# Attention over the kept tokens, one core: the first batch's side work in other slots, batch six's output products over three slots, the last pair's short chunk second and its outputs chunk by chunk

## The chip, the core and the metric

The kernel runs on one core of one Trainium2 chip. The metric is the device time in microseconds of one execution. Every number below comes from three timed executions of the kernel before the change, or from one profiled execution of it, in which each instruction and each DMA packet carries a time.

The engines are named as in the profile: PE (matrix multiplication; PEld is its weight load), DVE (vector), ACT (scalar, with the exponentials), POOL (general, here mostly the issuer of indirect DMAs) and SP (which only issues DMAs). Each works through its own list of instructions in order; semaphores tie the lists together.

## The reference

Eight batches of 512 features by 1024 tokens, eight heads of 64 features, a 0/1 mask over the tokens that keeps about half of them:

```
xt = transpose(x, (0, 2, 1))
q = xt @ Wq.T
qh = q.reshape(B, T, 8, 64).transpose(0, 2, 1, 3)
scores = scale * einsum('bhqd,bhkd->bhqk', qh, qh)
logits = (scores * cmask + (1.0 - cmask) * NEG) * rmask
attn = softmax(logits, axis=-1)
ctx = einsum('bhqk,bhkd->bhqd', attn, qh)
out = ctx.transpose(0, 2, 1, 3).reshape(B, T, D) @ Wo.T
return x + transpose(out, (0, 2, 1))
```

Query, key and value are the same projection. A masked token attends to all tokens alike, so all masked tokens of a batch have one output row. Only the kept tokens (at most 536 here) and one row for the mean have to be computed.

## The kernel before

**Tiling.** Per batch the tokens are turned into rows in DRAM (`turn`: a DVE transpose of a quarter of the batch, then four DMAs by SP). The rank of each kept token is looked up (`search`, DVE), the kept rows are gathered by indirect DMA (`gather`, POOL), and PE transposes them back into feature-major form (`collect`, five chunks, copied out of PSUM by DVE or ACT). `add_features` sums features on ACT. The heads go in pairs, four pairs per batch, 32 pairs in all, written here as (batch, pair). A pair's 536 tokens are four long chunks of 128 and a short one of 24, number 4, called `LAST`.

**The loop.** For each pair there are five slots, c = 0 to 4. A slot issues `scores` of its chunk (PE, then ACT's exponentials with a running sum: two of 128x536 for a long chunk, the tiles `e`, two of 128x268 for the short one, the tile `el`), then the products of earlier chunks' exponentials with the values (`weigh`, PE, tiles `av`), and side work that a table puts there: `put(batch, pair, slot, task, rank)`. Tasks of a slot with a rank below 0 come before `weigh`, those from 0 to 5 after it, those from 5 up last. The engines' lists keep this order.

**Side work that the change moves.** For the pair after the one running: `project` (queries), `turn_values` (values through PE and two copies by DVE), `square` (ACT) of the values, `top_of` (DVE: the sums of the squares, `len`, and their maximum, `top`), `bias_of` (PE spreads `top`, DVE makes of it the bias that the next pair's exponentials need). So in slot 4 there is a chain: square (ACT), len and top (DVE), top (PE), bias (DVE), first exponential of the next pair (ACT).

**The gate.** `open_slot` and `pass_gate` make the first `weigh` of a slot wait for the first noted read of a PSUM bank since the slot before, or else for the slot's own first exponential. In slot 4 that is mostly the short chunk's first `el`.

**PSUM.** The pool tag "t" has two banks, used in turn by nearly all side work of PE; the scores have two tiles of two banks ("s"), the products with the values two banks ("av").

**Outputs.** A batch's output is made by seven half-size products after Strassen's scheme (`half_product` k = 1 to 7, tiles `ph`) and a plain one for the short chunk (`output`). DVE combines them into `side` and `joined` tiles, reading `ph` out of the "t" banks; `joined_0` and `joined_1` are the two halves of the rows and go to DRAM (`od`) by POOL's DMAs. Later POOL fetches all 1024 tokens' rows with indirect DMAs that add to the input rows (`fetch`, eight per batch, blocks i = 0 to 7), DVE transposes each block (`finish_blocks`, tile `whole`) and SP stores it. For batch five the fetches stand in the slots of pair (7,0) and the blocks in those of (7,1); for batch six everything stands in (7,1) to (7,3).

**The end.** The last batch's outputs are plain products, four per chunk, one per pair. Three of the four (`begin_output`) stand in the last pair's slots 3 and 4 and are kept in SBUF as partial sums; after the last pair `end_output` adds the fourth on DVE and stores the chunk. `fetch_last` gathers the eight blocks from `od`, and `finish_tokens` transposes them on PE, adds x on DVE, and stores.

Of the kernel before, what the change touches and what calls it, by code (L numbers as in the profile page):

```python
# [305 lines left out]
def attention_of_kept_tokens(ctx, tc, x, mask, wq, wo, out, ident, wqT, woT, verdict, flag):  # L306
# [416 lines left out]
    def weigh(pair, c, cross):  # L723
# [7 lines left out]
        for r in range(2):  # L731
            rows = slice(r * DK, (r + 1) * DK)
            hf = r ^ cross
            for h in range(2):
# [5 lines left out]
                    stop=(c == LAST),  # L740
# [3 lines left out]
    def weigh_behind(pair, before, c):  # L744


        cross = c in (2, 4)
# [236 lines left out]
    def last_products(b, i, prs, po):  # L984

        n = max(Q, sizes[i])
        for pr in prs:
            first, last = pr == prs[0], pr == prs[-1]
# [19 lines left out]
    def begin_output(b, i):  # L1008
# [5 lines left out]
        partials[i] = pa  # L1014

# [71 lines left out]
    def fetch(b, i):  # L1087
        nc.gpsimd.indirect_dma_start(  # L1088
            out=gs[b, i],
            out_offset=None,  # L1090
            in_=ods[b],
# [242 lines left out]
    def plan():  # L1334
# [15 lines left out]
        for p, (b, pr) in enumerate(pairs[:-1]):  # L1350
# [4 lines left out]
            put(b, pr, 3, squares, ahead, rank=0)  # L1355
# [3 lines left out]
        for n in range(1, B):  # L1359
            if n == 1:  # L1360
                turns = [(0, 0, 0), (0, 0, 1), (0, 0, 3), (0, 0, 4)]
                finds = [(0, 1, 0), (0, 1, 3), (0, 1, 3), (0, 1, 4), (0, 2, 0)]
                feats = [None] * (ND + 2) + [(0, 0, 4), (0, 1, 0)]
                takes = finds
                means, mean = (0, 2, 1), (0, 2, 3)
                turned = [(0, 2, 3)] * NC
            else:
                b = n - 2
                if n == 2:
                    loads = [(0, 1, i) for i in range(NC)] + [(0, 2, i) for i in range(3)]  # L1370
                    turns = [(0, 2, 3), (0, 2, 4), (0, 3, 1), (0, 3, 3)]
                    feats = [(0, 2, 3)] * 2 + [(0, 2, 4)] * 2
# [19 lines left out]
            for i in range(NQ):  # L1392
                put(*turns[i], turn, n, i, rank=6.8 if turns[i][2] == LAST - 1 else 1)
# [3 lines left out]
            for i in range(NC):  # L1397
                put(*finds[i], search, n, i, rank=4.6 if n > 1 and finds[i][2] == LAST else 0)
# [8 lines left out]
        for b in range(B - 1):  # L1407
# [3 lines left out]
            if b == B - 3:  # L1411
                steps = ((1, 2), (6, 5, LAST + P), (7, 3, 4))
            elif b == B - 2:
                steps = ((1, 2, 6, 5, 4, 7, 3, LAST + P),)
            for i, step in enumerate(steps):
                for k in step:
                    task, k = (output, k - P) if k > P else (half_product, k)
                    put(*at[i], 3, task, b, k, rank=7.1)
                    if b == B - 2 and task is half_product and k == 5:
                        for j in (2, 3):  # L1420
                            put(*at[i], 3, mix_contexts, b, j, rank=7.1)
# [5 lines left out]
            else:  # L1427
                for k in range(2):
                    put(nxt, 1, 1 + k, mix_contexts, b, k, rank=5.5)
            if b < B - 3:  # L1430
# [23 lines left out]
        last = B - 1  # L1454
        for i in (LAST, 0, 1, 2):
            put(last, 3, 3 + (i == 2), begin_output, last, i, rank=7)
        for k in range(ND):
            put(*((0, 3, 1), (0, 3, 2), (0, 3, 3), (1, 1, 2))[k], mix_weights, k, rank=5.5)
# [10 lines left out]
    def late(n):  # L1469
# [41 lines left out]
        for p, pair in enumerate(pairs):  # L1511
# [3 lines left out]
            for c in range(NC):  # L1515
# [159 lines left out]
```

## Time and profile before

| | us |
|---|---|
| median of three executions | 635.94 |
| lowest, highest | 634.38, 639.89 |
| profiled execution, whole | 637.8 |
| profiled execution, its span from first to last instruction | 635.8 |
| PE busy | 591.4 (93%) |
| DVE, ACT, POOL busy | 404.7, 348.2, 253.1 |
| mean granted PE clock | 0.974 |

In the steady middle of the run a batch takes 69.6 us (the eight half products of one step start at 182.72, 252.74, 322.12 and 391.97). PE's list has almost no idle time there. Idle time of another engine costs nothing as long as PE does not wait for it. PE idles in five places: before 39 us (loading and ranking), in the slots of batch 0 (39 to 103 us), at batch five's and six's outputs (521 to 580 us), in the last pair (580 to 613 us), and at the end, when the last rows are fetched.

### The profile page before, as it was taken

The page shows a single profiled execution, that of the slowest core. Times are in us where ns is not written, and L with a number is a line of the kernel's source. Part 1 is how long each engine was busy: PE and PEld are TensorE (multiplying, and loading weights), DVE is VectorE, ACT ScalarE, POOL GpSimd, SP SyncE. Part 2 cuts the span into 40 slices and gives each one's busy share as a digit, 9 for nine tenths or more (in the row PEclk, how much of TensorE's full clock was granted, in tenths as well). Part 3 has the DMA queues.
Part 4 walks back from the last instruction along what each step waited for, and adds up shares of the span by engine and source line. Part 5 has one row for each costly group of instructions (what it writes and reads, how often), then busy time and mean ns, then how long its engine had stood idle before and what let it go on. Part 6 is the DMA issues. An engine that isn't in the chain of part 4 may idle for free.

```text
span 635.8 us, 22524 instructions
## 1 busy us (share of the span) xinstructions
PE 591.4 (93%) x9296; PEld 447.1 (70%) x9296; DVE 404.7 (64%) x1191; ACT 348.2 (55%) x986; POOL 253.1 (40%) x363
## 2 busy tenths in 40 slices
PE   6689989999999999999999999999999998898964
PEld 4557756678877787788877877788777876685432
DVE  6546768766575777757875677667765663665343
ACT  5366667666556566566556665567555545435300
POOL 4501333410245525445255534543445525528021
PEclk9799979999999999999999999999999999999985
DMA  8746535432457867886888867886766667788737
GB/s 271 243 129 190 201 99 146 139 117 82 142 174 195 221 134 239 274 221 131 234 252 237 178 149 226 266 228 128 191 196 147 134 164 191 148 268 158 168 121 220
DMA packets 100152, 116.80 MB, mean 184 GB/s; under 512 B 13224, under 2 KB 67048, under 8 KB 100040
## 3 DMA queue, kind: packets, MB, share of 16 engines
q1 hardware_dynamic: 76176, 76.56, 40.9%
q0 software_dynamic: 19520, 36.58, 25.2%
q10 hardware_dynamic: 4344, 2.12, 1.1%
q8 instruction: 75, 1.23, 0.8%
q14 instruction: 37, 0.30, 0.2%
HBM read 72.68 MB, written 42.54 MB: 181 GB/s over the span
## 4 chain that ended last, share of the span: by engine, by line
PE 74%; DMA 9%; DVE 6%; issue 4%; POOL 2%; ACT 2%; SPq 1%; DVEq 0%; POOLq 0%; ACTq 0%
PE av L735 18%; PE s L688 17%; PE pq L554 15%; PE ph L934 12%; PE v L592 3%; PE xc L495 2%; DMA g<-od,origin 2%; PE s L702 2%; DMA od<-joined 2%; PE pa L991 2%; POOL g L1088 1%; DVE joined L958 1%; PE po L878 1%; ACT e L711 1%; DMA x<-in_x_dram 1%
## 5 line engine op out<-in xcount | busy, mean ns | idle before, releaser
L711 ACT ACTIVATE e<-s,bias 128x536 f32<-128x536 f32 x256 | 178.1, 700 | 55.5 <-PE s L688 54.1
L735 PE MATMUL av<-e,v 64*64 64x268 f32 x2048 | 169.2, 392 | 8.4 <-ACT el L711 5.5
L688 PE MATMUL s<-qT 64*64 64x268 f32 x2048 | 168.8, 391 | 0.8 <-issue 0.6
L554 PE MATMUL pq<-xc,wqT 64*64 64x268 f32 (+1 forms) x1984 | 134.8, 388 | 0.1
L735 PEld LDWEIGHTS av<-e,v 64*64 64x64 f32 x2048 | 89.5, 133 | 44.9 <-ACT el L711 8.8
L688 PEld LDWEIGHTS s<-qT 64*64 64x64 f32 x2048 | 100.0, 133 | 24.1 <-ACT e L711 4.4
L554 PEld LDWEIGHTS pq<-xc,wqT 64*64 64x64 f32 x1984 | 97.3, 134 | 20.5 <-DVE m L641 0.8
L826 POOL DMA_DIRECT2D row<-rt x120 | 63.7, 554 | 98.6 <-DVE rt L823 95.7
L1088 POOL DMA_INDIRECT g<-od,origin x48 | 77.4, 1613 | 20.8 <-issue 15.0
L482 POOL DMA_INDIRECT xin<-xd,source x40 | 39.4, 984 | 58.4 <-PE av L735 18.9
L601 DVE COPY v<-v 128x320 f32<-128x320 f32 x64 | 28.4, 486 | 46.2 <-PE v L592 46.2
L711 ACT ACTIVATION_READ_ACCUMULATOR e<-s,bias 128x1 f32 x256 | 50.1, 196 | 0.0
L934 PE MATMUL ph<-wo,mix 128*128 128x256 f32 x168 | 39.5, 383 | 2.3 <-DVE joined L958 2.3
L464 DVE TENSOR_SCALAR_CACHE_REDUCE junk<-rank,key 128x1024 f32<-128x1024 f32 (+4 forms) x40 | 39.9, 997 | 2.6 <-DMA rank<-ranks 2.6
L711 ACT ACTIVATE el<-s,bias 128x268 f32<-128x268 f32 x64 | 30.3, 480 | 19.6 <-PE s L702 19.2
L427 ACT ACTIVATE junka<-x 128x512 f32<-128x512 f32 x64 | 40.2, 628 | 0.7
L958 DVE TENSOR_TENSOR joined<-ph,side 128x512 f32<-128x512 f32 x28 | 19.1, 684 | 32.3 <-PE ph L934 32.3
L1058 DVE STREAM_TRANSPOSE whole<-g 128x512 f32<-128x512 f32 x56 | 36.6, 684 | 4.5 <-DMA g<-od,origin 4.5
L769 ACT COPY cT<-av 128x268 f32<-128x268 f32 x62 | 22.0, 383 | 29.2 <-PE av L735 29.2
L934 PEld LDWEIGHTS ph<-wo,mix 128*128 128x128 f32 x168 | 30.5, 190 | 9.2 <-DVE joined L958 2.7
L975 POOL DMA_DIRECT2D od<-joined x14 | 10.9, 776 | 63.7 <-DVE joined L958 63.5
L401 DVE STREAM_TRANSPOSE xt<-x 128x1024 f32<-128x1024 f32 x28 | 34.2, 1224 | 0.2
(180 smaller groups left out, 816.0 us busy)
## 6 DMA issues: line engine op xcount, KB each, us to landing
xd<-xt SPq DMA_DIRECT2D x120, 128.0 KB
x<-in_x_dram SPq DMA_DIRECT2D x56, 256.0 KB
g<-xd SPq DMA_DIRECT2D x48, 256.0 KB
out_dram<-whole SPq DMA_DIRECT2D x20, 512.0 KB
rb<-row SPq DMA_DIRECT2D x60, 160.0 KB
od<-joined POOLq DMA_DIRECT2D x14, 512.0 KB
out_dram<-whole SPq DMA_DIRECT2D x16, 256.0 KB
rank<-ranks SPq DMA_DIRECT2D x7, 512.0 KB
```

The source lines that it names most:

```text
L401: nc.vector.transpose(xt.rearrange("p k (d f) -> p k d f", d=ND), xs[b][r][:, :, at : at + n].rearrange("p d (k t) -> p k d t", t=Q),)
L427: nc.scalar.activation(junk, xs[b][r][:, d, :], AF.Copy, accum_out=xbars[b][:, d, r : r + 1])
L464: nc.vector.tensor_scalar(junk[:, :n], rank[:, i * P :], key[:, col], 0.0, ALU.is_le, ALU.add, accum_out=found[:, col])
L482: nc.gpsimd.indirect_dma_start(out=xin[:n, :], out_offset=None, in_=rows_of_x[b], in_offset=bass.IndirectOffsetOnAxis(ap=searches[b][2][:n ...
L554: mm = nc.tensor.matmul(pqs[pair][hf][heads[h], :n], wqT[rows, d, at : at + DK], xcs[b][rows, d, hf * KH : hf * KH + n], start=(not cross ...
L688: nc.tensor.matmul(s[h][to, hf, :KH], qT[heads[h], at : at + DK], qT[heads[h], hf * KH : (hf + 1) * KH], start=True, stop=True,)
L711: act = nc.scalar.activation(e[:, h], of[h], AF.Exp, bias=biases[pair][:, c : c + 1], scale=SCALE, accum_out=acc[:, h, c : c + 1],)
L735: mm = nc.tensor.matmul(avs[pair][hf][heads[h], :KH], v[rows, c, heads[h]], e[rows, h, hf, :] if c < LAST else e[rows, h, :], start=(c == ...
L826: nc.gpsimd.dma_start(row[:, :, a, :].rearrange("h c j -> (h c) j"), rt[a * Q : a * Q + 2 * NC, :])
L934: nc.tensor.matmul(po[:, t * m : (t + 1) * m], left[:, i, t * P : (t + 1) * P], right[:, i, :], start=(i == 0), stop=(i == 1),)
L1058: nc.vector.transpose(whole.rearrange("p (d a) n -> p a d n", a=A)[:, :, :, i * Q : (i + 1) * Q], gs.pop((b, i)).rearrange("p (a d f) -> p ...
L1088: nc.gpsimd.indirect_dma_start(out=gs[b, i], out_offset=None, in_=ods[b], in_offset=bass.IndirectOffsetOnAxis(ap=origin[:, b, i : i + 1] i ...
```

## The change

The last pair's loop runs the short chunk second, and everything after the loop is written anew:

```diff
-            for c in range(NC):
+            for c in (0, LAST, 1, 2, 3) if final else range(NC):
...
         last = pairs[-1]
+        first, second = (open_output(B - 1, i) for i in range(2))
+        last_products(B - 1, 0, range(2), first, ends=False)
+        weigh(last, LAST - 1, 1)
+        inv = inverses(last)
+        begin_output(B - 1, LAST)
+        last_products(B - 1, 0, [2], first, starts=False, ends=False)
         open_slot()
-        weigh_behind(None, last, 0)
-        spread(last, inverses(last))
-        begin_output(B - 1, LAST - 1)
+        for k in (LAST - 2, LAST - 1):
+            weigh(last, k, 0)
+        spread(last, inv)
+        last_products(B - 1, 1, range(ND - 1), second, ends=False)
         end_values_last(last)
+        last_products(B - 1, 0, [ND - 1], first, starts=False)
+        store_output(B - 1, 0, first)
+        end_output(B - 1, LAST, "t")
+        last_products(B - 1, 1, [ND - 1], second, starts=False)
+        store_output(B - 1, 1, second)
...
-        for j, i in enumerate((LAST, 0, 1, 2, 3)):
-            end_output(B - 1, i, ("t", "av")[j % 2])
...
+        for i in range(2, LAST):
+            po = open_output(B - 1, i)
+            last_products(B - 1, i, range(ND), po)
+            store_output(B - 1, i, po)
```

So chunks 0 to 3 are summed over all four pairs in PSUM (tag "s"), without partial sums; chunk 0 and 1 are open while the last values are made, chunks 2 and 3 follow whole. The copy out of PSUM moves from DVE to ACT:

```diff
+    def store_output(b, i, po):
+        oc = sb.tile([P, D], F32, tag="oc", name=f"oc_{b}_{i}", bufs=ND)
+        nc.scalar.copy(oc, po)
+        nc.sync.dma_start(place_outputs(b)[places[i], :], oc)
```

A fetch of a batch other than the first names only the rows that its block can need, so that it depends only on the stores of those rows:

```diff
+        rows = min(NK, END + (i + 1) * P) if b else NK
...
-            in_=ods[b],
+            in_=ods[b][0:rows, :],
```

Batch six's products go from one slot into three, (7,0), (7,1) and (7,2), slot 3 each. Its fetches and blocks are put anew; the first two blocks' transposes move from slot 0 of (7,3) to slot 3 of (7,2):

```diff
-                steps = ((1, 2, 6, 5, 4, 7, 3, LAST + P),)
+                steps = ((1,), (2, 6, 5, LAST + P, 3), (4, 7))
+                at = [(nxt, 0), (nxt, 1), (nxt, 2)]
...
-                slots = [(2, 1), (2, 1), (2, 2), (2, 3), (2, 4), (3, 0), (3, 0), (3, 1)]
+                slots = [(2, 0), (2, 0), (2, 4), (3, 0), (3, 0), (3, 1), (3, 1), (3, 2)]
...
-                ends = [(nxt, 3, c) for c in (0, 0, 3, 3, 3, 3, 3, 3)]
+                ends = [(nxt, 2, 3)] * 2 + [(nxt, 3, 3)] * (NT - 2)
```

In batch 0 the squares of pairs (0,0), (0,1) and (0,3) go from slot 3 to slot 4, behind the short chunk's exponentials; one turn and one search go behind the bias; searches, sums, turns and two weight mixes go to other slots:

```diff
+            short = b == 0 and pr != 2
+            put(b, pr, LAST if short else 3, squares, ahead, rank=-1 if short else 0)
...
+                turns = [(0, 2, 2), (0, 2, 4), (0, 3, 1), (0, 3, 2)]
+                feats = [(0, 2, 0), (0, 2, 1)] + [(0, 2, 4)] * 2
```

**ACT at the end of pair (0,0), before.** `e_0_3` are the exponentials of chunk 3, `el_0_4` those of the short chunk, `sq_1` the squares for pair (0,1), `mixed_rank` a copy for the token ranks, `junka` a sum over features:

```order
L711 ACTIVATE e_0_3_659,sums_86<-s_0_3_0_660,bias_0_537 128x536
L711 ACTIVATE e_0_3_659,sums_86<-s_0_3_1_661,bias_0_537 128x536
L608 ACTIVATE sq_1_680<-v_1_634 128x640
L1297 COPY mixed_rank<-rank_mixed_t 64x128
L711 ACTIVATE el_0_4_694,sums_86<-s_0_4_695,bias_0_537 128x268 x2
L427 ACTIVATE junka_6_720,xbar_464<-x_1_375 128x512
```

The same place now:

```order
L711 ACTIVATE e_0_3_659,sums_86<-s_0_3_0_660,bias_0_537 128x536
L711 ACTIVATE e_0_3_659,sums_86<-s_0_3_1_661,bias_0_537 128x536
L1310 COPY mixed_rank<-rank_mixed_t 64x128
L711 ACTIVATE el_0_4_692,sums_86<-s_0_4_693,bias_0_537 128x268 x2
L608 ACTIVATE sq_1_700<-v_1_634 128x640
L427 ACTIVATE junka_6_718,xbar_464<-x_1_375 128x512
```

The squares have moved behind both short exponentials; in (0,1) and (0,3) likewise, without the copy.

**DVE in slot 3 of pair (7,2), now.** `v_3` are the copies of the next pair's values, `whole<-g_0` and `whole<-g_1` the first two fetched blocks of batch six, `ph_4` and `ph_7` its last two products, `len_3` the sums of squares:

```order
L918 TENSOR_TENSOR mix_2_8608<-cT_0_7242 128x512
L601 COPY v_3_8635<-v_3_0_8636 128x5x64
L601 COPY v_3_8635<-v_3_1_8637 128x5x64
L1070 STREAM_TRANSPOSE whole_8688<-g_0_8274 128x4x4x32
L1070 STREAM_TRANSPOSE whole_8688<-g_1_8298 128x4x4x32
L971 TENSOR_TENSOR side_6_8419<-ph_4_8691,side_6_8419 128x512
L962 TENSOR_TENSOR joined_1_8696<-ph_7_8698,side_5_8426 128x2x256
L962 TENSOR_TENSOR joined_1_8696<-ph_7_8698,side_6_8419 128x2x256
L614 TENSOR_REDUCE len_3_8722<-sq_3_8686 128x10
```

Before, nothing stood between `v_3` and `len_3`: the joins stood in (7,1), the two blocks behind slot 0 of (7,3).

**POOL from (7,1) on, before.** `od` are the output rows of batch six, `row` the inverse sums on their way to DRAM, `g` the fetched blocks:

```order
L975 DMA od_8445<-joined_1_8436 128x2x512
L975 DMA od_8445<-joined_0_8412 128x2x512
L890 DMA od_8445<-oc_4_8454 24x128 x4
L826 DMA row_1_8572<-rt_1_8570 10x32 x4
L1088 DMA g_0_8267<-od_8445,origin 128x512
L1088 DMA g_1_8291<-od_8445,origin 128x512
L1088 DMA g_2_8337<-od_8445,origin 128x512
```

The same place now:

```order
L894 DMA od_8448<-oc_4_8429 24x128 x4
L979 DMA od_8448<-joined_0_8412 128x2x512
L830 DMA row_1_8555<-rt_1_8553 10x32 x4
L1101 DMA g_0_8274<-od_8448,origin 128x512
L1101 DMA g_1_8298<-od_8448,origin 128x512
L979 DMA od_8448<-joined_1_8696 128x2x512
L1101 DMA g_2_8344<-od_8448,origin 128x512
```

The second half's store has moved behind the first two fetches, and the six other fetches stand behind it.

More of the change, by code (lines that the diff above doesn't have):

```diff
@@ L739, in weigh @@
                     start=(c == 0 and first),
-                    stop=(c == LAST),
+                    stop=bool(not cross and c == LAST - 1) if pair == pairs[-1] else c == LAST,
                 )
@@ L744, in weigh_behind @@
     def weigh_behind(pair, before, c):
+        if c and pair == pairs[-1]:
+            for k in {LAST: (0,), 1: (0,), 2: (LAST, 1), 3: (1, 2)}[c]:
+                weigh(pair, k, c in (1, 3))
+            return
         cross = c in (2, 4)
```

36 lines of the change are left out of this document (16 added, 20 removed).

## The prediction

> **What bounds the kernel now.** The page comes first.
>
> ```profile
> PE 591.4 (93%) x9296; PEld 447.1 (70%) x9296; DVE 404.7 (64%) x1191; ACT 348.2 (55%) x986; POOL 253.1 (40%) x363
> ```
>
> PE is the bound, and the change leaves its work alone (the same matrix products, in another order). So it can only win or lose PE's waits, a slowed clock, and the tail after PE's last product. PE's timeline is read next, for the places that the change touches. Columns: start, duration, what; in brackets the idle time before it and what ended that.
>
> ```profile
> 52.38 0.30 PE L632 MATMUL top<-ident,top 64*64 64x64 f32 x8
> 62.12 0.81 PE L592 MATMUL v<-ident,qT 64*64 64x64 f32 x40 [0.38 <-DVE qm L578]
> 66.50 1.14 PE L735 MATMUL av<-e,v 64*64 64x268 f32 x16 [0.94 <-ACT el L711]
> 67.57 0.34 PE L632 MATMUL top<-ident,top 64*64 64x64 f32 x8
> 70.55 0.75 PE L735 MATMUL av<-e,v 64*64 64x268 f32 x8
> 81.77 1.76 PE L495 MATMUL xc<-ident,xin 128*128 128x128 f32 x12 [1.13 <-DVE xc L498]
> 85.22 2.06 PE L735 MATMUL av<-e,v 64*64 64x268 f32 x16 [0.68 <-ACT el L711]
> 87.06 0.44 PE L632 MATMUL top<-ident,top 64*64 64x64 f32 x8
> 91.55 0.63 PE L735 MATMUL av<-e,v 64*64 64x268 f32 x8
> 101.84 1.13 PE L735 MATMUL av<-e,v 64*64 64x268 f32 x16 [1.00 <-ACT el L711]
> 102.80 0.29 PE L632 MATMUL top<-ident,top 64*64 64x64 f32 x8
> ```
>
> In batch 0 PE waits in slot 4 for the short chunk's exponential. Pair (0,2) is slow besides: from the gate to `top` it takes 1.84 us where (0,1) takes 1.07, from `top` to the next `av` 4.49 against 2.98. That is the clock, in the windows (PE busy is the second number, the granted clock stands ahead of the last two):
>
> ```profile
> 80.20:83.61 3.41, 2.20 (x21) 1.52 (x22) 3.38 (x6) 2.65 (x8) 2.48 (x14) 1.00 0.60 191
> 83.61:90.44 6.83, 6.16 (x64) 3.10 (x64) 3.04 (x12) 3.89 (x14) 0.00 (x0) 0.50 0.40 110
> 554.60:558.01 3.41, 1.71 (x8) 1.53 (x9) 1.89 (x3) 0.00 (x0) 0.00 (x0) 1.00 0.15 49
> ```
>
> Half the clock for 6.83 us, after a stretch with the collection's transposes and the wait of 1.13 us. At batches five and six and at the end, on PE, DVE and POOL:
>
> ```profile
> 535.94 1.13 PE L735 MATMUL av<-e,v 64*64 64x268 f32 x16 [1.10 <-ACT el L711]
> 556.30 1.99 PE L934 MATMUL ph<-wo,mix 128*128 128x256 f32 x8 [2.31 <-DVE joined L958]
> 579.21 1.13 PE L735 MATMUL av<-e,v 64*64 64x268 f32 x16 [1.10 <-ACT el L711]
> 580.28 1.09 PE L688 MATMUL s<-qT 64*64 64x268 f32 x16
> 604.55 1.31 PE L794 MATMUL rb<-ident,ris 128*64 128x128 f32 x20
> 609.57 3.60 PE L991 MATMUL po<-woT,cT 128*128 128x512 f32 x8
> 617.77 2.33 PE L1105 MATMUL o<-ident,g 128*128 128x128 f32 x8 [4.60 <-DMA g<-od,origin]
> ...
> 554.96 0.71 DVE L1058 STREAM_TRANSPOSE whole<-g 128x512 f32<-128x512 f32 x1 [1.34 <-DMA g<-od,origin]
> 593.53 0.71 DVE L1058 STREAM_TRANSPOSE whole<-g 128x512 f32<-128x512 f32 x1 [0.79 <-DMA g<-od,origin]
> 600.28 0.17 DVE L807 TENSOR_TENSOR sums<-sums,share 128x10 f32<-128x10 f32 x1 [6.04 <-ACT el L711]
> ...
> 530.73 1.03 POOL L826 DMA_DIRECT2D row<-rt  x2 [2.70 <-issue]
> 533.20 1.69 POOL L1088 DMA_INDIRECT g<-od,origin  x1 [1.45 <-DMA od<-joined]
> 573.76 1.67 POOL L1088 DMA_INDIRECT g<-od,origin  x1 [0.59 <-DMA out_dram<-whole]
> 586.84 1.56 POOL L1088 DMA_INDIRECT g<-od,origin  x1 [0.30 <-issue]
> 614.18 1.00 POOL L1079 DMA_INDIRECT g<-od,origin  x1 [25.78 <-DVE flag L1568]
> ```
>
> The wait at 556.30 looks like a DVE matter, but DVE itself waited until 554.96 for the last block of batch five to land, with the join behind it. The chain that ended last gives the landings:
>
> ```profile
> 520.76 11.60 DMA od<-joined
> ...
> 613.99 2.00 DMA od<-oc
> ...
> 623.03 5.47 DMA g<-od,origin
> ```
>
> **The first batch.** ACT and DVE in slot 4:
>
> ```profile
> 50.50 0.73 ACT L608 ACTIVATE sq<-v 128x640 f32<-128x640 f32 x1
> 51.12 0.25 ACT L1297 COPY mixed_rank<-rank_mixed_t 64x128 f32<-64x128 f32 x1
> 65.25 0.73 ACT L608 ACTIVATE sq<-v 128x640 f32<-128x640 f32 x1
> 65.88 0.48 ACT L711 ACTIVATE el<-s,bias 128x268 f32<-128x268 f32 x1
> 66.51 0.81 DVE L614 TENSOR_REDUCE len<-sq 128x10 f32<-128x640 f32 x1
> 67.36 0.16 DVE L621 TENSOR_REDUCE top<-len 128x1 f32<-128x10 f32 x1
> 79.89 1.25 DVE L401 STREAM_TRANSPOSE xt<-x 128x1024 f32<-128x1024 f32 x1
> ```
>
> Pair (0,1): ACT comes free at 65.25. With the squares behind, the gate opens 0.63 us sooner, but `top` comes later: two short exponentials (2 x 0.48), squares 0.73, len 0.85 (66.51 to 67.36), top and the step to PE 0.25 make 2.8, so 68.05 instead of 67.57: **+0.5**. The wait only moves from `av` to `top`. Pair (0,0): from 50.50, with the copy (0.25), about 53.6 against 52.38; with the copy's own product late by a little, **+1.3**; of this the wait of 0.38 at 62.12, for DVE, takes back **-0.4**. Pair (0,3): +0.5 by the same sum, and a turn (1.25) and a weight mix now stand before the value copies that open slot 3's gate; DVE has some slack there, so I take +0.4 (between 0 and 1): **+0.9**.
>
> Pair (0,2) keeps its squares. The turn at 79.89 leaves the place between the collection's first product and its copy, and two feature sums leave ACT: of the 1.13 us some 0.1 to 0.3 stay, **-1.0**. If the clock then holds, the rows above give 0.77 + 1.51 = 2.3 us, and half of the busy 6.16 would be 3.1: I take **-2.8**. Sum of the first batch: 1.3 - 0.4 + 0.5 + 0.9 - 1.0 - 2.8 = -1.5.
>
> The Trainium skill (TensorE: Matmul & The Clock Gate, Part 1) has the clock halved only after an idle window of about 3.4 us. The trace does not agree: the 3.41 us before the drop had 2.20 busy. By that rule no clock would be lost before or after, and this term would be nil.
>
> **Batch six's products.** Each takes about 1.8 us of PE wherever it stands (the row at 556.30 has 1.99 with an end that overlaps the next). In (7,0) product 1 fills the wait of 1.10 at 535.94; its copy by ACT leaves some 0.25. In (7,1) two products instead of three now stand ahead of the wait at 556.30. The blocks of batch five land a little sooner, as fetch 0 no longer needs the second half's store: at most POOL's 1.45, and POOL was busy with `row` until 531.76, so 1.2. The wait stays at about 2.2 (PE comes 0.9 later to the slot, with 1.8 less to do, the blocks 1.2 sooner), and some 0.7 follow for the last product and `top`. In (7,2) products 4 and 7 fill the 1.10 at 579.21, but the joins stand behind two blocks. The pair starts some 4 us sooner, 3.6 of it for the two products moved out of (7,1), so fetch 0 (today 573.76) leaves POOL at 569.8, fetch 1 at 571.7, landing 4.5 later (first landing at the end: 614.18 to 617.77, 3.6; last one 5.47), so the joins end near 579, and the gate and `top` wait 1.5. Waits before 1.10 + 2.31 + 1.10 = 4.5, after 0.25 + 2.2 + 0.7 + 1.5 = 4.7: **0**, with 3 us to either side, as each hangs on a landing. The last pair starts near 580.3 as before.
>
> **The last pair.** Today PE reaches the `rb` products 24.3 us after the pair's start (580.28 to 604.55), with nine long products ahead of them. Three stay ahead; six at 0.90 (3.60 for four) go behind: 18.9 with today's waits, less some of those, 17.5: 597.8. But `rb` needs the sums, and on DVE these stand behind batch six's blocks. `joined_1` is stored from 579.2. Landing: between 2.00 (half the bytes) and 11.60 (the same store among others); twice 2.00 = 4.0 is nearest, since batch five's stores to the output are done by then. With 0.4 for POOL's step (0.84 at 533.20 after that landing, at most) fetch 2 stands at 583.6, five more at 1.87 (573.76 to 586.84 by seven): fetch 7 at 592.9. Landing: between 3.6 and today's 6.7 (586.84 to 593.53), I take 6.0: 598.9. Transpose 0.71 and the sums' five small steps at some 0.18 (600.28): `rb` at 600.5, a wait of 2.7 that is not there today.
>
> By the Trainium skill (DMA: Bandwidth & Descriptors, Anatomy of one DMA; 2.0 us and the bytes by 436e3) 512 KB take an estimated 3.2 us instead of 4.0, and the end comes 0.8 sooner; no row here shows such a store alone.
>
> From `rb` on: 1.31, then thirteen long products at 0.90 (11.7) and the short one's 0.45: PE ends at 614.0, against 613.17 today (609.57 + 3.60). ACT's copy (0.6, from 0.73 for the squares' 640 columns), the store 2.00 and POOL's 0.4: fetch 3 at 617.0, since chunks 0 to 2 are out long before. Today all eight fetches run from 614.18 to 623.03, 1.26 apart; then four follow fetch 3: 622.0, **-1.0**. Five in a row instead of eight: the fifth lands after about 4.7 (from 3.6 for the first to 5.47 for the eighth), **-0.8**. The rest of the tail is the same.
>
> **Sum.** -1.5 + 0 - 1.0 - 0.8 = -3.3 on the profiled execution (637.8 with its span of 635.8). The median of three is 635.94, 1.9 lower, and their spread of 5.5 us is larger than the term. The difference goes on the median: **632.6 us**.
>
> **The rivals.**
> - The last blocks land before PE needs the sums. The wait of 2.7 is gone, and with a quicker (7,2) another 0.5: 629.4. For it: PE's arrival at 597.8 and the end of the sums at 600.5 are close. Against it: six fetches at 1.87 behind a store cannot be hurried.
> - The clock still drops in (0,2). The new collection still has five chunks of transposes and small waits in one stretch, and the slot's gate (0.6) follows. The two quoted stretches differ the wrong way round (2.20 busy: drop; 1.71: none), so transposes seem to weigh little. The Trainium skill says so too (the same page, Part 4: transposes are not counted as busy in the same way), and the trace bears it out that far. Then 2.8 come back: 635.4.
> - Slower: the second half's store lands late, as the one at 520.76 did. With 11.60 for 4.0 the fetches, the sums and `rb` come 7.6 later: 640.2. It decides from a landing of block seven after some 602.2 (3.3 later than forecast). For it: the very row. Against it: at 520.76 four 512 KB stores and loads were under way, here few. With a late (7,2) on top it passes 642.
> - The change does not do what it says: naming fewer rows frees no fetch early. Then batch five's wait keeps its 1.2: 633.8.
>
> **Chances.** Forecast 0.50 (629.5 to 635), early blocks 0.22, clock 0.13, late store 0.12, rows 0.03. A measurement of this kernel tells 1% (6.4 us) from no change. Faster by more (below 629.6) are three quarters of the early case (0.17) and a fifth of the forecast's (0.10): 0.27. Slower by more (above 642.3): half of the late store and a rest of 0.03: 0.09. Else 0.64. The range, 627 to 639.5, leaves out the worst of the late store and the best of the early case.
>
> **What would show it.** In (0,0), (0,1) and (0,3) `av` in slot 4 no longer waits for `el`, and `top` waits 1 to 1.7 us for DVE. The granted clock stays at 1.00 from 30 us to the tail. The wait before product 5 is still there at 2 us. In the last pair `rb` waits for DVE, with `whole` before it waiting for `g`. The last fetch leaves 1 us sooner than now or more. The forecast is wrong if `top` does not wait, if the sums are ready before PE, or if the joins wait long for blocks 0 and 1.

## The result and the profile after

The changed kernel takes 642.69 us (median of 20 executions, 638.90 to 647.83), the kernel before 636.32 us on the same chip (20 executions, 633.39 to 641.61). The ratio is 1.0092, with a 95% interval of 1.0069 to 1.0115: 5.9 us slower by the ratio, 6.4 us by the medians. The forecast was 632.6 us, between 627.0 and 639.5.

The profiled execution of the changed kernel took 645.6 us (span 643.5), 2.9 more than its median and 7.8 more than the profiled one of before. PE's instructions are as many as before (9296); its busy time grew by 3.4 us (from 591.4), in part by a slower clock:

```profile
PE 594.8 (92%) x9296; PEld 446.7 (69%) x9296; DVE 402.7 (63%) x1187; ACT 349.3 (54%) x986; POOL 254.9 (40%) x363
```
The starts of the pairs (by the first `top` product ahead of each, in PE's timeline) divide its span:

| stretch | before, us | after, us | difference | forecast |
|---|---|---|---|---|
| start to (0,0) | 39.33 | 40.05 | +0.72 | 0 |
| (0,0) | 13.05 | 14.69 | +1.64 | +0.9 |
| (0,1) | 15.19 | 15.37 | +0.18 | +0.5 |
| (0,2) | 19.49 | 20.56 | +1.07 | -3.8 |
| (0,3) | 15.74 | 16.31 | +0.57 | +0.9 |
| (1,0) to (6,3) | 418.73 | 419.75 | +1.02 | 0 |
| (7,0) to (7,2) | 58.64 | 58.81 | +0.17 | 0 |
| (7,3) to the end | 55.63 | 57.96 | +2.33 | -1.8 |

(In the forecast the 0.38 us that the wait for `qm` gave back stood with (0,0).) First the first batch, in PE's timeline of the changed kernel (start, duration, what, idle time before it and what ended that):

```profile
54.74 0.34 PE L632 MATMUL top<-ident,top 64*64 64x64 f32 x8 [1.83 <-DVE top L621]
67.96 1.14 PE L735 MATMUL av<-e,v 64*64 64x268 f32 x16 [0.69 <-ACT el L711]
70.11 0.34 PE L632 MATMUL top<-ident,top 64*64 64x64 f32 x8 [1.01 <-DVE top L621]
83.37 0.65 PE L495 MATMUL xc<-ident,xin 128*128 128x128 f32 x4 [0.35 <-DVE xc L498]
85.63 1.40 PE L495 MATMUL xc<-ident,xin 128*128 128x128 f32 x8 [1.60 <-DMA xin<-xd,source]
88.83 2.06 PE L735 MATMUL av<-e,v 64*64 64x268 f32 x16 [0.69 <-ACT el L711]
104.84 1.13 PE L735 MATMUL av<-e,v 64*64 64x268 f32 x16 [0.69 <-ACT el L711]
106.98 0.34 PE L632 MATMUL top<-ident,top 64*64 64x64 f32 x8 [1.01 <-DVE top L621]
```

`top` waits for DVE in all three pairs, as foreseen. But the gate's wait has only shrunk from 0.94 and 1.00 to 0.69, not gone. In (0,2) the collection's wait of 1.13 is down to 0.35, and behind it stands a new one of 1.60, for a gathered chunk. POOL's timeline tells why it is late: the fourth gather (78.94; before, it left at 69.24) now stands behind `row`.

```profile
76.53 2.11 POOL L830 DMA_DIRECT2D row<-rt  x4 [8.45 <-DVE rt L827]
78.94 1.01 POOL L482 DMA_INDIRECT xin<-xd,source  x1 [0.30 <-issue]
```

The windows are stretches of 3.41 us, cut where the clock can change (the last section says how that was found). Busy PE is the second number, the granted clock the third from the right. They show the clock halved here as before, and a second time near the end:

```profile
82.64:86.05 3.41, 1.46 (x12) 0.98 (x10) 3.32 (x5) 0.71 (x2) 0.00 (x0) 1.00 0.71 229
86.05:89.46 3.41, 2.60 (x22) 1.24 (x24) 0.00 (x0) 2.09 (x7) 2.41 (x14) 0.50 0.60 165
89.46:92.88 3.42, 3.42 (x44) 2.02 (x40) 1.27 (x7) 1.32 (x5) 0.29 (x2) 0.50 0.00 0
604.88:608.29 3.41, 0.86 (x16) 0.89 (x18) 1.34 (x6) 0.00 (x0) 0.00 (x0) 1.00 0.54 144
608.29:611.70 3.41, 3.41 (x12) 1.54 (x8) 2.15 (x7) 0.75 (x2) 0.00 (x0) 0.50 0.89 229
```

Batch seven's first pairs and the last one, on PE, DVE and POOL, with one row of the chain that ended last (start, time from issue to landing):

```profile
538.69 0.83 PE L688 MATMUL s<-qT 64*64 64x268 f32 x9 [1.56 <-issue]
555.63 1.99 PE L938 MATMUL ph<-woT,cT 128*128 128x256 f32 x8
583.93 1.13 PE L735 MATMUL av<-e,v 64*64 64x268 f32 x16 [1.24 <-DVE joined L962]
585.54 0.34 PE L632 MATMUL top<-ident,top 64*64 64x64 f32 x8 [0.47 <-DVE top L621]
585.68 1.17 PE L688 MATMUL s<-qT 64*64 64x268 f32 x16
603.59 1.13 PE L735 MATMUL av<-e,v 64*64 64x268 f32 x16
607.43 1.62 PE L798 MATMUL rb<-ident,ris 128*64 128x128 f32 x20 [2.71 <-DVE ris L818]
608.99 5.04 PE L995 MATMUL po<-woT,cT 128*128 128x512 f32 x8
618.81 3.60 PE L995 MATMUL po<-woT,cT 128*128 128x512 f32 x8
...
605.88 0.71 DVE L1070 STREAM_TRANSPOSE whole<-g 128x512 f32<-128x512 f32 x1 [2.99 <-DMA g<-od,origin]
...
598.16 7.69 DMA g<-od,origin
...
630.89 0.95 POOL L1091 DMA_INDIRECT g<-od,origin  x1 [0.30 <-issue]
```

The `rb` products wait 2.71 us for DVE's `ris`, behind the last block's transpose (605.88), whose fetch took 7.69 us to land. Behind that wait the clock is halved for one window: `rb` takes 1.62 us for 1.31, and eight long passes take 5.04 us where the eight at the end take 3.60. The 1.56 us at 538.69, in (7,0), is a wait for which the profile names no cause.

### The profile page after: what moved, and what is told of

Read it like the earlier page. It is cut to its first block, busy times and chain, and to the rows that moved or that the text cites. A ratio compares the mean times of both kernels' runs of the same rounds, so it can differ in the third digit from the quotient of the medians.

```text
span 643.5 us, 22510 instructions
## 1 busy us (share of the span) xinstructions
PE 594.8 (92%) x9296; PEld 446.7 (69%) x9296; DVE 402.7 (63%) x1187; ACT 349.3 (54%) x986; POOL 254.9 (40%) x363
## 3 DMA queue, kind: packets, MB, share of 16 engines
q1 hardware_dynamic: 76176, 76.56, 40.1%
## 4 chain that ended last, share of the span: by engine, by line
PE 69%; DMA 9%; DVE 7%; issue 6%; POOL 4%; SPq 2%; ACT 2%; POOLq 0%; DVEq 0%; ACTq 0%
PE av L735 16%; PE s L688 15%; PE pq L554 14%; PE ph L938 11%; DMA g<-od,origin 3%; PE xc L495 3%; PE v L592 3%; POOL g L1101 2%; PE s L702 2%; PE po L995 2%; DMA xd<-xt 1%; DVE joined L962 1%; DMA od<-joined 1%; DMA x<-in_x_dram 1%; PE po L882 1%
## 5 line engine op out<-in xcount | busy, mean ns | idle before, releaser
L554 PE MATMUL pq<-xc,wqT 64*64 64x268 f32 (+1 forms) x1984 | 133.4, 386 | 0.0
L735 PEld LDWEIGHTS av<-e,v 64*64 64x64 f32 x2048 | 87.8, 133 | 46.6 <-ACT el L711 5.1
```

What stands on the lines that cost most here:

```text
L554: mm = nc.tensor.matmul(pqs[pair][hf][heads[h], :n], wqT[rows, d, at : at + DK], xcs[b][rows, d, hf * KH : hf * KH + n], start=(not cross ...
L735: mm = nc.tensor.matmul(avs[pair][hf][heads[h], :KH], v[rows, c, heads[h]], e[rows, h, hf, :] if c < LAST else e[rows, h, :], start=(c == ...
```

## The experiments

Ratios are to the kernel before on the same chip in the same session; the brackets hold the 95% interval. A session is what ran together on one chip; the median of the kernel before was between 636.25 and 642.48 us in them, so times of different sessions are not compared, only their ratios.

**The three parts, each alone on the kernel before.** `first_alone` has the first batch's table entries and squares, `six_alone` batch six's products, slots and the fetches' rows, `last_alone` the loop's order and all behind it.

```diff
# first_alone
+            short = b == 0 and pr != 2
+            put(b, pr, LAST if short else 3, squares, ahead, rank=-1 if short else 0)
...
+                takes = [(0, 1, 0), (0, 1, 2), (0, 1, 3), (0, 2, 0), (0, 2, 0)]
...
+                    turns = [(0, 2, 2), (0, 2, 4), (0, 3, 1), (0, 3, 2)]
...
# six_alone
+            in_=ods[b][0:rows, :],
...
+                steps = ((1,), (2, 6, 5, LAST + P, 3), (4, 7))
...
# last_alone
+            for c in (0, LAST, 1, 2, 3) if final else range(NC):
...
```

> The kernel before with the first batch's part alone (turns, feature sums, searches, gathers, squares, weight mixes). Theory: this part costs the 3.5 us that the trace shows between the first pair's start and batch one (pair by pair +1.6, +0.2, +1.1, +0.6), so 3.5 us slower than the kernel before; the gathered chunk's wait in pair (0,2) and the half clock behind it are in its trace. Rival: the part is worth what was forecast (-1.5 us), and the 3.5 are the chance of one execution (its start was 0.7 late as well); then 0 to 1.5 us faster.

> The kernel before with batch six's part alone: products, mixes, fetches, joins and blocks in the new slots, and the rows named in the fetches. Theory: the waits before product 5 and in the short chunks go, and as much comes back in pair (7,2); 0 us, between -1 and +1. As the tail is the old one, DVE has the blocks of batch six ahead of the last sums, so a wait ahead of the last rb products is possible, but there six long products stand behind it. Rival: these slots are what costs the last 3 us; then 2 to 3 us slower.

> The kernel before with the last pair's part alone: short chunk second, outputs by chunks, no partial sums through SBUF. Theory: as in the changed kernel, rb waits for DVE behind batch six's blocks and the clock drops to half for 3.41 us behind that wait; with batch six's fetches later than in the changed kernel the wait is longer, so 3 to 5 us slower than the kernel before. Rival: the last pair by itself gains the 1.8 us forecast, and only its meeting with the new slots of batch six costs; then 1 to 2 us faster.

Measured: `first_alone` 1.0109 [1.0065, 1.0153], `six_alone` 1.0005 [0.9979, 1.0031], `last_alone` 0.9964 [0.9930, 0.9999]. So the first batch costs more than either side expected, 7.0 us (2.8 to either side, from six executions); batch six's part is even; and the last pair by itself gains 2.3 us, against the theory. In its trace `rb` does not wait, since batch six's fetches leave in their old slots, the last of them 5.9 us after the pair's start instead of 12.6:

```profile
600.59 1.13 PE L735 MATMUL av<-e,v 64*64 64x268 f32 x16
601.65 1.31 PE L798 MATMUL rb<-ident,ris 128*64 128x128 f32 x20
602.89 3.70 PE L995 MATMUL po<-woT,cT 128*128 128x512 f32 x8
```

The stretch from (7,3) to the end is 52.99 us there, for 55.63 before and 57.96 in the changed kernel. `six_alone`, with the old tail, takes 55.56. The loss of 2.33 in the last pair is thus made where the two parts meet.

**The meeting.** `after_again` is the changed kernel itself, `first_undone` (and once more `undone_again`) the changed kernel with the first batch as before. `sums_first` and `undone_sums` add to these two a move of three blocks on DVE, from ahead of the last pair's sums to behind them:

```diff
-                ends = [(nxt, 2, 3)] * 2 + [(nxt, 3, 3)] * (NT - 2)
+                ends = [(nxt, 2, 3)] * 2 + [(nxt, 3, 3)] * 3
...
         inv = inverses(last)
+        for i in range(5, NT):
+            finish_blocks(B - 2, i)
+        while stores[0] or stores[1]:
+            issue_stores()
```

> The changed kernel with three of batch six's blocks (the last three) moved on DVE from ahead of the last pair's sums to behind them. Theory: the 2.7 us wait of rb goes, and with it the half clock of 3.41 us that follows (1.7 us, as the window before holds work again), less what the later chain takes back: 3.5 to 4.5 us faster than the changed kernel, about 2 us slower than the kernel before; rb starts 19 us after the pair's start and the clock stays at 1.00 to the tail. Rival 1: the clock drop has another cause, and only the wait's 2.7 us go. Rival 2: the blocks' landing moves the wait to the products of cT behind; then under 1 us faster.

> The changed kernel itself, beside the others of this call. Theory: the sum of the parts run alone (first batch +6, batch six 0, last pair -2.5) and of their meeting in the last pair (rb waits 2.7 us and the clock is halved for 3.41 us behind it, together 4.4): 6 to 8 us slower than the kernel before. Rival: its 6.4 us were those of one chip, and here it is slower by 3 us or less.

> The changed kernel with the first batch's part as before. Theory: what is left is batch six's part (0), the last pair's gain (-2.6) and the meeting of the two (+2.7 of wait and +1.7 of clock): 1 to 2 us slower than the kernel before, 5 to 6 us faster than the changed one. Rival: the last pair's parts still gain 2 us with batch six's new slots, so the first batch carries all of the loss; then 1.5 to 2.5 us faster than the kernel before.

> The changed kernel with the first batch's part as before and, besides, three of batch six's blocks moved on DVE from ahead of the last pair's sums to behind them. Theory: rb no longer waits and the clock behind it holds, so 3.5 to 4.5 us faster than the same kernel without the move, and 2 to 3 us faster than the kernel before. Rival: the wait is gone but the time comes back in the last fetches; then under 1 us between the two.

> Once more the changed kernel with the first batch's part as before, beside a kernel that has the last pair's part with the old slots of batch six. Theory: batch six's new slots turn the last pair's gain into a loss, because rb then waits 1.5 to 2.7 us for DVE: 4 to 6 us slower than last_turns, 1 to 3 us slower than the kernel before. Rival: the difference between the two lay in their chips; then less than 2 us between them.

Measured: `after_again` 1.0107 [1.0073, 1.0141], `first_undone` 1.0041 [1.0012, 1.0069] and `undone_sums` 1.0003 [0.9979, 1.0028], all in one session; `sums_first` 1.0091 [1.0058, 1.0123] in the session of `first_alone`; `undone_again` 1.0031 [1.0000, 1.0062] beside 0.9953 for a kernel with the same last pair and the old slots of batch six. The latter is `last_turns`, further below, which also keeps two of the first batch's moves. That is 5 us between the two on one chip, so the rival of the chips falls. `after_again` and `first_undone` differ by the first batch's part alone, and put it at 4.2 us in their session, less than the 5 to 6 expected and the 7.0 of `first_alone`. In `undone_again` the wait and what follows it, in PE's timeline, then the same place in `undone_sums`:

```profile
601.12 2.40 PE L798 MATMUL rb<-ident,ris 128*64 128x128 f32 x20 [2.79 <-DVE ris L818]
603.45 5.61 PE L995 MATMUL po<-woT,cT 128*128 128x512 f32 x8
```

```profile
598.53 1.31 PE L798 MATMUL rb<-ident,ris 128*64 128x128 f32 x20
599.78 3.70 PE L995 MATMUL po<-woT,cT 128*128 128x512 f32 x8
```

Moving three transposes removes the wait of 2.79 and the 3.0 us of slow products behind it (2.40 + 5.61 against 1.31 + 3.70). In time it is worth 0.38% (1.0041 to 1.0003, intervals that overlap), 2.4 us, less than the 3.5 to 4.5 expected, and `undone_sums` is level with the kernel before instead of 2 to 3 us faster. In the profiled `first_undone` the wait was 1.55 and no half clock followed, so the price differs from execution to execution. In the trace of `sums_first` `rb` does not wait either, and (7,3) to the end takes 53.41 us for the changed kernel's 57.96. Its time stayed 3.8 us above what was expected, about as much as the first batch alone cost more in that session than was expected of it (7.0 for 3.5).

`fill_wait` leaves the wait and puts work into it, whose result nobody reads:

```diff
+        fill = bank("fill")
+        for i in range(2):
+            nc.tensor.matmul(fill, cTs[B - 1, 0][:, :P], plain(0), start=True, stop=True)
         spread(last, inv)
```

> The changed kernel with two long products whose result nobody reads (1.8 us of PE) in the wait of rb in the last pair. Theory: the clock is halved after a window of 3.41 us with little product work; with the wait filled the clock stays at 1.00 from rb to the tail, rb's products take 1.31 us instead of 1.62 to 2.40 and the eight behind them 3.7 instead of 4.0 to 5.0: 1 to 1.7 us faster than the changed kernel, though PE does more, and 5 us slower than the kernel before. Rival: the clock has another cause (the waits of the other engines, or the transfers); then it drops as before, and the time is that of the changed kernel or up to 0.5 us more.

Measured: 1.0122 [1.0079, 1.0166]. In its trace `rb` does not wait and the clock stays at 1.00 from 594.4 us to the tail. In this trace, then, the half clock goes when the idle time is filled, as the theory has it. A gain in time is not shown: it is 7.8 us slower than the kernel before for the 5 expected, but the session holds no run of the changed kernel, and `first_alone` alone cost 1.1% in another session.

**The first batch.** `squares_back` is `first_alone` without the squares' move; `squares_alone` is that move and nothing else (the first two lines of the diff of `first_alone`).

> The kernel before with the first batch's part but its squares, which stay in slot 3 ahead of the short exponentials. Theory: the squares carry 3.0 us of the first batch's loss (top's waits of 1.83, 1.01 and 1.01 us for DVE, less 0.27, 0.25 and 0.31 off the gate's), and the rest is the wait for the gathered chunk (0.4 to 1.6) less 0.8 at the collection: within 1.5 us of the kernel before. Rival: the gathers and turns are what costs, and the squares are even; then 4 us slower or more.

> The kernel before with one edit: the squares of pairs (0,1), (0,2) and (1,0) go behind the short exponentials of slot 4 in the pair before. Theory: the gate opens only 0.3 us sooner (it is the short product that ACT waits for, not the squares), and top waits 1.8, 1.0 and 1.0 us for DVE instead: 3 us slower than the kernel before, or 3 to 5 with a window of half clock now and then. Rival: with the other tasks at their old places the squares come out even (the waits of first_alone come from the searches and turns that stand with them); then within 1 us.

Measured: `squares_back` 1.0022 [0.9992, 1.0051], `squares_alone` 1.0033 [1.0002, 1.0064], against 1.0109 for both; the three are of different sessions. The intervals are as wide as the differences, so the times alone do not settle what the squares cost, but the traces are plain. In `squares_back` the collection waits 0.35 us and no `top` waits in the batch. With the squares behind, slot 4 of (0,1) reads like this on ACT, DVE and PE (`after_again`):

```profile
66.18 0.48 ACT L711 ACTIVATE el<-s,bias 128x268 f32<-128x268 f32 x1 [0.57 <-PE s L702]
67.11 0.73 ACT L608 ACTIVATE sq<-v 128x640 f32<-128x640 f32 x1
...
67.88 0.82 DVE L614 TENSOR_REDUCE len<-sq 128x10 f32<-128x640 f32 x1 [1.89 <-ACT sq L608]
...
66.81 1.13 PE L735 MATMUL av<-e,v 64*64 64x268 f32 x16 [0.69 <-ACT el L711]
68.95 0.34 PE L632 MATMUL top<-ident,top 64*64 64x64 f32 x8 [1.01 <-DVE top L621]
69.11 2.02 PE L688 MATMUL s<-qT 64*64 64x268 f32 x16
70.84 2.88 PE L554 MATMUL pq<-xc,wqT 64*64 64x268 f32 x32
```

ACT is idle for 0.57 us before `el`: with the squares gone it is the short product that it waits for, so the gate's wait is only 0.25 us shorter (0.94 to 0.69), and PE then waits 1.01 us for `top`. And the next products run at half speed: 2.02 us where 1.12 is usual. The windows of that execution:

```profile
65.77:69.19 3.42, 1.72 (x36) 0.76 (x32) 1.18 (x3) 1.67 (x5) 0.94 (x1) 1.00 0.95 268
69.19:72.60 3.41, 3.41 (x40) 2.40 (x36) 2.76 (x13) 1.65 (x5) 0.00 (x0) 0.50 0.61 234
99.91:103.32 3.41, 1.71 (x34) 0.69 (x29) 0.98 (x2) 2.28 (x7) 0.00 (x0) 1.00 0.83 184
103.32:106.73 3.41, 3.41 (x40) 2.29 (x40) 2.72 (x11) 1.59 (x5) 0.17 (x1) 0.50 0.75 259
```

The waits of 0.69 and 1.01 in one window leave half of it idle, and the next window runs at half clock, in (0,1) and again in (0,3). From (0,0) to (1,1) this execution takes 80.1 us, `first_undone` 74.5. The 5.6 between them are 3.0 of waits (1.83 - 0.27, 1.01 - 0.25, 1.01 - 0.31), less 0.8 at the collection (1.13 to 0.35), and 3.4 for two half windows.

`fill_top` puts long products that nobody reads into those waits, two in (0,0), one each in (0,1) and (0,3):

```diff
         pts = [bank(f"top_{nm}_{r}") for r in range(2)]
+        for r in range({(0, 1): 2, (0, 2): 1, (1, 0): 1}.get(pair, 0)):
+            nc.tensor.matmul(pts[0], ident, wqT[:, 0, :], start=True, stop=True)
```

> The changed kernel with long products whose result nobody reads ahead of top's products in slot 4 of pairs (0,0) (two, 1.8 us), (0,1) and (0,3) (one each, 0.9 us), that is in the waits for the squares. Theory: these waits of 1.01 us, with the 0.69 ahead of them, leave about 1.7 us of work in a window of 3.41 and halve the clock for the next one; filled, the clock stays at 1.00 from 40 to 125 us and the waits vanish into work: the same time at full clock, 1 to 2 us less than the changed kernel, so 4.5 to 5.5 us slower than the kernel before. Rival: the clock falls there for another reason (as it did in the one execution of the kernel before that was profiled); then the same half windows remain and the time is the changed kernel's.

Measured: 1.0105 [1.0071, 1.0138], no gain that can be seen (the changed kernel had 1.0107 in its own session). Its trace shows that the idea holds: the windows behind the filled waits stay at full clock. Why it did not pay is open. In the profiled execution the gathered chunk came 1.96 us late and the clock fell there for two windows, but at 648.9 us this is the longest of nine, 5.6 above their median.

```profile
65.90:69.30 3.40, 2.71 (x31) 1.15 (x27) 1.14 (x6) 2.31 (x7) 1.49 (x2) 1.00 0.86 262
69.30:72.70 3.40, 3.40 (x58) 2.45 (x60) 2.52 (x12) 1.54 (x5) 0.00 (x0) 1.00 0.81 291
...
85.75 0.63 PE L495 MATMUL xc<-ident,xin 128*128 128x128 f32 x4 [1.96 <-DMA xin<-xd,source]
```

**What beats both kernels.** `mended` is the changed kernel with the squares in slot 3 and the three blocks behind the sums. `last_table` is `last_alone` with the first batch's part but its squares; `last_table_rows` adds the fetches' rows; `last_turns` is `last_alone` with only the line of `turns` above and the feature sums that go with it; `last_again` is `last_alone` in another session.

> The changed kernel with its squares back in slot 3 and three of batch six's blocks behind the last pair's sums on DVE, all else as changed. Theory: without top's waits (3.0 us and the half windows behind them) and without rb's (2.7 and the half window) it is 6 to 8 us faster than the changed kernel, within 1.5 us of the kernel before, on the faster side. Rival: the collection, the turns and batch six's slots cost besides; then it stays 2 us slower than the kernel before or more.

> The kernel before with the last pair's part and with the first batch's without its squares; batch six as before. Theory: the last pair's 2.6 us and up to 1 us at the collection of pair (0,2): 2 to 3.6 us faster than the kernel before. Rival: the gain of the last pair alone was within its interval's noise; then within 1 us of the kernel before.

> As last_table, with the fetches of batches one to six naming only the rows that they can reach. Theory: fetch 0 of batch five no longer waits for the second half's store (1.45 us), batch five's blocks land sooner and the wait ahead of product 5 falls by 1.2 us: 1 us faster than last_table. Rival: that wait moves to the step behind it, or batch six's fetches are late for another reason; then no difference.

> The last pair's part alone on the kernel before, once more beside other runs. Theory: the gain of 2.3 us (ratio 0.9964) was real: 1.5 to 3.5 us faster than the kernel before. Rival: the gain is within noise; then less than 1 us either way.

> The kernel before with the last pair's part and, of the first batch's, only the turns and feature sums of batch two in their new slots; searches, gathers, squares and weight mixes as before. Theory: the last pair's 2.5 us (ratio 0.9936 to 0.9964 alone) and the collection's wait in pair (0,2) from 1.13 down to 0.35, 0.8 us, without the gathers that land late: 3 to 5 us faster than the kernel before, with no half clock between 40 and 125 us. Rival: the turn in slot 2 of (0,2) holds up the value copies behind it on DVE; then no better than the last pair alone, 2 to 3.5 us faster.

Measured: `mended` 0.9991 [0.9961, 1.0021], `last_table` 0.9986 [0.9957, 1.0014], `last_table_rows` 1.0001 [0.9971, 1.0031], `last_again` 0.9936 [0.9904, 0.9969] (632.93 us for 637.17), `last_turns` 0.9953 [0.9926, 0.9980] (633.54 for 636.37). The last pair's part alone beats the kernel before, by 2.3 and 4.1 us in two sessions, and with it the changed kernel. `mended` comes out level, as expected. With the new turns the collection's wait falls to 0.34 us as expected, but no gain on top of the last pair's can be told (3.0 us faster in all). `last_table_rows` was to be 1 us faster than `last_table` and is not; its rival holds. `last_table` fell short of its 2 to 3.6 us: in its profiled execution pair (0,1) lost 1.64 us that `squares_back`, with the same table in another session, did not lose. It is not one execution alone: `first_alone`, `sums_first`, `last_table` and `last_table_rows`, all with this table and from the two sessions in which the kernel before took over 642 us, have (0,1) at 16.77 to 17.17 us, nearly all of it at full clock (`fill_wait`, from there too, has a half window in it); the five profiles with the table in other sessions have 14.92 to 15.37, and `squares_alone`, `six_alone` and `last_alone`, without it in the long sessions, 15.12 to 15.71. That may be part of why the first batch cost 7.0 us in one session and 4.2 in another. In `last_table` ACT and DVE stand still there for 1.66 and 2.41 us, and the profile names no engine or DMA of this core that releases them; what does is open.

## Why the prediction was wrong

The forecast missed the profile by 11.0 us (+7.7 for -3.3; the median by 10.1): 5.0 in the first batch, 4.1 in the last pair, 0.2 in batch six, 1.7 outside the change.

- **The first batch's clock, -2.8.** This step failed first. It took the half clock of one profiled execution for a cost that the kernel always pays, and let the change remove it. Of twelve traces of kernels with the squares in slot 3 (seven of them with the first batch wholly as before), that one alone has a half window between 40 and 125 us: there was mostly nothing to gain. Of six traces with the squares moved and their waits unfilled, five have one or two, four of them behind a window that holds a wait of `top`, and the changed kernel's own behind the gathered chunk's: the change makes what it was to remove.
- **The collection, -1.0.** The wait itself shrank as forecast (1.13 to 0.35, and 0.34 to 0.35 in the experiments). What the step left out is a moved instruction's queue: the fourth gather went past `row` on POOL, and what then ended the wait was its landing. That cost 1.60 in the changed kernel's profile, 1.96 in `fill_top`, 0 in `after_again`.
- **The squares, +1.3, +0.5 and +0.9.** The direction and `top`'s waits were right. "The gate opens 0.63 us sooner" was not: 0.25 and 0.31, as ACT was not the last to come. The waits' net is 3.0 us, and the half windows come on top.
- **Batch six, 0.** Right as a sum (+0.17 in the profile, 1.0005 alone), in part by luck. Naming fewer rows did what it was to do: fetch 0 of batch five left 10.5 us after the start of (7,0) instead of 11.7 and waited for no store. The wait ahead of product 5, put at 2.2, was none in this execution (555.63) and 2.13, 1.05 and 0.35 in others; the joins' wait, put at 1.5, was 1.24 + 0.47; and the 1.56 in (7,0) was not forecast at all.
- **The last pair, -1.8.** The wait of `rb` was forecast at 2.7 and is 2.71, for the reason given; its size was right by luck, as both its ends came 1.5 later after the pair's start than forecast: the last fetch landed after 7.69 us instead of 6.0, and PE came at 19.0 us instead of 17.5. The step that failed is the wait's price: it was counted once, and the half clock behind it was not: from `rb` to PE's end 15.0 us instead of 13.5. Another 0.5 is the last fetch (8.5 us after PE's end for 8.0), and 0.6 what follows it: from the last fetch to the end it is 12.6 us for 12.8, a fall of 0.2 instead of 0.8.
- **The rivals.** The slower rival (640.2, a late store) named the right place and the right sign: block seven's late landing holds up `rb`. Its reason was wrong: the store was not late (the fetch behind it left 2.8 us after the pair's start, for 3.3 forecast), the last fetch's own landing was. And it gave the wait alone as the price. The clock rival (635.4) came true in the profiled execution: (0,2) has its two half windows still, though behind the wait for the gathered chunk. With it the first batch comes to +1.3 instead of -1.5, for 3.5 measured; no rival had half windows behind the waits that the change itself moves.
- **The signs.** The waits of `top` and of `rb` for DVE came as foretold. The others did not: `av` still waited for `el` (0.69), the clock fell twice before the tail, the wait ahead of product 5 was gone, and the last fetch left 7.9 us later than before instead of 1 us sooner.
- **What lay outside.** The start (+0.72) and batches one to six (+1.02) are within what differs without the change. In the traces of all these kernels the first pair starts anywhere between 38.8 and 40.1 us, whatever the kernel, and outside the two long sessions batches one to six take between 418.5 and 421.5.

Without the wait of 2.7 the forecast's sum for the last pair would have been -4.5; alone the part measured -2.3 and -4.1.

## What to carry to other kernels

In these traces a wait of PE costs its own length and, where it leaves PE idle for half of a window of the clock, half of the next window too, sometimes of the next two; so two waits that stand close together can be dearer than the same two apart, and a wait that is only moved can cost more at its new place. Before a cost in one trace is counted as a gain, look for it in a second execution. A step that is moved to a later slot is to be followed on each queue that it enters, the issuing engine's above all: in the changed kernel's profile one gather behind a row store, and five small sums behind six blocks, gave back more than the moves had won.

## What the runs showed of the hardware

**The clock's rule.** Within a trace the changes of the clock lie on a grid of 3.413 us: the two drops of the changed kernel's profile, at 86.05 and 608.29, are 153 steps apart. Of all windows on that grid at full clock, between 36 and 612 us in the 19 traces, 24 have less than 1.74 us of busy PE, and 22 of them are followed by half clock. Of the 58 with 1.76 to 2.34 us, one is: that of the kernel before, quoted in the prediction, 2.20 us with many transposes. So the point lies near half a window, whatever the wait's cause, and where the grid falls decides whether a given wait pays. Getting the clock back takes more: of the half-clock windows in the same stretch, the four with 2.3 to 2.8 us of busy PE were followed by a second one, the 21 with 3.0 or more were not. The drop in (0,2), which lasts two windows both before and after the change, is such a case (2.75 and 2.60). The Trainium skill (TensorE: Matmul & The Clock Gate, Part 1) has a free-running window of 3413 ns, with which the grid agrees; it has the clock fall after an idle window, and there the traces differ, since 1.7 us of work in the window do not hold it. The Trainium skill (the same page, Part 4) does not count transposes as busy in the same way; the one exception seemed to agree, but the traces do not bear that out. In `squares_alone`, `undone_sums` and `six_alone` a window at the same place holds 2.20 to 2.29 us of the collection's transposes and nothing else, and the clock stays, as in the two rows of `squares_alone` below. Why it fell in the kernel before's profile is open.

```profile
83.59:87.00 3.41, 2.20 (x18) 1.55 (x16) 3.33 (x7) 2.65 (x7) 2.17 (x13) 1.00 0.61 166
87.00:90.41 3.41, 2.71 (x52) 1.70 (x55) 1.65 (x5) 2.98 (x10) 0.00 (x0) 1.00 0.58 155
```

The other stretch that the prediction quotes, 554.60 with 1.71 busy and no drop, was cut 0.05 us off the grid; its window holds 1.77.

**The same kernel in two sessions.** `last_alone` and `last_again` are one kernel. From (1,0) to (7,0) their profiled executions differ by 6.0 us (424.7 and 418.7), nearly all of it in the first pairs of the batches, in gaps of PE that the profile puts down to "issue" (1.06 us in (3,0) and 0.25 in (4,0) of `last_alone`) or to nothing. The kernel before took 642.48 and 637.17 us in those sessions. The same holds for every kernel here: this stretch takes 423.7 to 425.5 us in all eight traces of the two sessions in which the kernel before took over 642 us, and 418.5 to 421.5 in the other eleven.
